# Two transformer layers on one core: where the reciprocal roots of the second attention's norms are computed

## The chip, the core and the metric

The kernel runs on one core of a Trainium2 chip, as one launch. A core has five engines with instruction queues of their own: TensorE (PE in the profile; its weight loads are PEld), VectorE (DVE), ScalarE (ACT), GpSimd (POOL) and SyncE (SP), and 16 DMA engines that all queues feed. Each engine works its queue in order, and engines wait for one another by semaphores. The metric is the device time of one execution in microseconds (us); lower is better. All data are 32-bit floats.

## What is computed

Two layers, each a cross attention and a mixture of experts, on x of 8 x 100 rows of 512, with a context of 8 x 722 rows. Cut to what matters here:

```
x = x + attention0(norm(x), context)            # 16 heads of 32, causal
x = x + experts0(norm(x))                       # 8 experts of 2048, 2 per row; has a norm of its own
x = x + attention1(norm(x), context)            # 16 heads of 64; has a norm of its own
x = x + experts1(norm(x))                       # 8 experts of 1024, 2 per row; a norm on its result
norm(x) = (x - mean(x)) / sqrt(var(x) + 1e-5)   # over the 512 columns of a row
```

Where a sublayer starts with a norm of its own, two norms follow each other on the same row. The kernel makes them in one: the variance after the first norm is known from that before it, so that the product of both factors is one reciprocal root, 1 / sqrt((1 + eps) var + eps^2).

## The kernel before

The 800 rows lie on the 128 partitions in seven tiles, the last with 32 rows (`NTILE`, `rows`, L20 and L71); x stays in SBUF throughout. The program is written in the order of the computation, a scheduler then places each engine's instructions, and that placed order is what the engines keep to.

A norm has three helpers. `moments` (L126) gives mean and variance of a tile by VectorE. `factors` (L134) makes r, the reciprocal root, and t = -mean x r: ScalarE's root (L139 for two norms in one, L141 for one), VectorE's reciprocal (L142), VectorE's product (L144). `scaled` (L147, L148) applies both to the tile on VectorE. `to_columns` (L155) turns the normed tile by TensorE (L159) and evicts it by ScalarE, plainly (L161) or with gain and shift (L168).

ScalarE looks a function up in a table, one set of which is in place at a time; where the next function needs another set, a table load stands before it (ACT_TABLE_LOAD in the trace). The root, the exponential, Gelu and Silu each bring a load when they follow one another; plain copies bring none.

Four places call `factors`. Those before the first attention (L572), before its experts (L638, L639) and on the last result (L1012) are not touched. The other two are:

- **The transition into the second attention (L732 to L744).** The experts' answers lie in DRAM in the order of experts. For each tile two gathers (`fetch`, L340, indirect DMAs that GpSimd issues) bring the two answers of each row into one of two buffers (`back0`, tag "nil"); VectorE adds them to x, weighted (L738); then come `moments`, `factors` and `scaled` (L742), the turned tile goes into `xT1` (L743), and GpSimd adds the output bias to x (L744). A gather may start when the buffer that it fills has been read. At the same time ScalarE and TensorE finish the early projections of the context (`project_early`, L725): projections (L432), their evictions by ScalarE (L436), turned values (L444, evicted at L446 to L449), and stores to DRAM that ScalarE's queue issues (L454, L464). Behind all this the first product of the attention (L760 by way of L421) needs the whole of `xT1`. One element of the last gathered tile, copied by GpSimd (L56), also holds back the loads of the next weights.
- **The second attention's output (`output`, L886).** The attention runs over 64 units, 8 batches x 8 pairs of heads. In a unit: keys projected from the context (L432, L436) or loaded, turned values (L444, L446), scores (`weighed`, L783: matmuls L793, row maximum L797 on VectorE, exponential with row sum L799 on ScalarE, reciprocal of the sums L804, spread by GpSimd L807 in the first three batches and through DRAM after them), the weights turned (`turned`, L815: L822 to L828) and the product (`attended`, L832: L843 and L847 to L850). The work is pipelined by one unit. The scores lie in two PSUM tiles, one for each head, each with a single buffer:

```python
scs = [ps_s.tile([T, 2, 512], F32, tag=f"sc{j}", name="ps_sc1") for j in range(2)]
```

so that the next unit's scores of a head can be written when the exponential of this unit has read them. When the units of all rows of a tile are done, a list of due steps (`due`, L910) puts three steps between units: `output` (product L891, sum L894, `moments`, `factors` and `scaled` into `xnf1`, L896), one unit later `logits1` (the tile turned, L159 and L161, and the router's matmuls L175), and one later `sent_on` (L903), which for groups of tiles picks the experts and sends the rows to them by indirect DMAs of GpSimd (L274). For the last two tiles no units are left to stand between.

Behind the attention, the choice of experts for the last group (L229 to L268), the order of the experts (L281 on) and the weights of the two answers (L948 to L952, with an exponential at L949) come before the experts' first rows arrive (L351). GpSimd adds the last norm's shift to x there (L1011).

Of the kernel before, what the change touches and what calls it, by code (L numbers as in the profile page):

```python
# [8 lines left out]
F32 = mybir.dt.float32  # L9
AF = mybir.ActivationFunctionType  # L10
ALU = mybir.AluOpType
AX = mybir.AxisListType

P = 128
# [15 lines left out]
EPS = 1e-5  # L30
# [36 lines left out]
def two_layers(ctx: ExitStack, tc: tile.TileContext, a: dict, out: bass.AP):  # L67
    nc = tc.nc
# [4 lines left out]
    const = ctx.enter_context(tc.tile_pool(name="const", bufs=1))  # L73
# [3 lines left out]
    def context(b, h):  # L77
        return a["ctxT"][:, b, h * (S // 2) : (h + 1) * (S // 2)].rearrange("(c p) s -> p c s", p=P)
# [9 lines left out]
    def of(layer, name, s, g):  # L88
        return lambda: a[name][bass.ds(owner[layer][s], 1), g].rearrange("o p j n -> (o p) j n")
# [13 lines left out]
    x = const.tile([P, NTILE, D], F32, name="x")  # L103
# [9 lines left out]
    eps = const.tile([P, 1], F32, name="eps")  # L113
    nc.vector.memset(eps, EPS)
    eps2 = const.tile([P, 1], F32, name="eps2")
    nc.vector.memset(eps2, EPS * EPS)
    rank = const.tile([P, NE], F32, name="rank")
    for e in range(NE):
        nc.vector.memset(rank[:, e : e + 1], float(NE - e))
# [6 lines left out]
    def moments(src, name):  # L126

        st = small.tile([P, 6], F32, tag="st", name=f"st_{name}")
        nc.vector.bn_stats(st, src)  # L129
        mv = small.tile([P, 2], F32, tag="mv", name=f"mv_{name}")  # L130
        nc.vector.bn_aggr(mv, st)
        return mv

    def factors(mv, tag, twice=False):  # L134


        r = small.tile([P, 1], F32, tag=f"r{tag}", name=f"r{tag}")
        if twice:
            nc.scalar.activation(r, mv[:, 1:], AF.Sqrt, bias=eps2, scale=1.0 + EPS)  # L139
        else:  # L140
            nc.scalar.activation(r, mv[:, 1:], AF.Sqrt, bias=eps)  # L141
        nc.vector.reciprocal(r, r)  # L142
        t = small.tile([P, 1], F32, tag=f"t{tag}", name=f"t{tag}")
        nc.vector.scalar_tensor_tensor(t, mv[:, :1], -1.0, r, ALU.mult, ALU.mult)  # L144
        return r, t

    def scaled(dst, src, r, t):  # L147
        nc.vector.tensor_scalar(dst, src, r, t, ALU.mult, ALU.add)  # L148
# [196 lines left out]
    def arrived(layer, e, r0, n, pool, psum, gamma=None, beta=None):  # L345

        xg = pool.tile([P, CAP // P, D], F32, tag="xg", name="xg")
        xT = pool.tile([P, DC, CAP], F32, tag="xgT", name="xgT")
        for s in range(-(-n // P)):
            w = min(P, n - s * P)  # L350
            nc.gpsimd.dma_start(out=xg[:w, s, :], in_=rows_of(sent, layer, e, r0 + s * P, w))  # L351
            to_columns(xT, xg[:, s, :], s * P, w, psum, gamma, beta, vector=True)
        return xT, xg
# [32 lines left out]
    def work_off(jobs, arrive, hidden, product, send_back, first=None, midway=None):  # L386


        (x, raw), done = arrive(*jobs[0][:3]), None
        if first is not None:  # L390
            weights.load(first + 8, raw[:1, 0, :1])
        for k, (e, r0, n, w1, w2) in enumerate(jobs):
            h = hidden(e, n, x, w1, lambda: done and send_back(*done))
            if k + 1 < len(jobs):
                x, raw = arrive(*jobs[k + 1][:3])
            if midway is not None and k == 4:
                midway(raw)
            done = e, r0, n, product(e, n, h, w2)
        send_back(*done)
# [71 lines left out]
    def columns_tile(name):  # L471
        return turned_x.tile([P, DC, NT], F32, tag="xT", name=name)
# [4 lines left out]
    with tc.tile_pool(name="a0", bufs=1) as ap, tc.tile_pool(name="a0w", bufs=3) as aw, tc.tile_pool(  # L477
        name="a0s", bufs=1, space=bass.MemoryType.PSUM
# [91 lines left out]
        for i in range(NTILE):  # L570
            xn = aw.tile([P, D], F32, tag="xn", name="xn0")
# [17 lines left out]
        for n in range(len(units) + 2):  # L589
            if n >= len(units) - B:  # L590
                next(steps)
            if n < len(units):
                c, b = units[n]
# [35 lines left out]
        for i in range(NTILE):  # L629
# [7 lines left out]
            mv = moments(x[:, i, :], "f0")  # L637
            scaled(xl[:, i, :], x[:, i, :], *factors(mv, "b", twice=True))  # L638
            r, t = factors(mv, "a")  # L639
# [34 lines left out]
    with f0, tc.tile_pool(name="f0w", bufs=2) as fw, tc.tile_pool(  # L674
        name="f0p", bufs=2, space=bass.MemoryType.PSUM
    ) as ps:
        cb = fp.tile([P, 2, DC, S // 2], F32, tag="xl", name="cb1")

        def fetch_context(behind):

            for h in range(2):
                nc.gpsimd.tensor_copy(cb[:1, h, 0, :1], behind[:1, 0, :1])
                nc.gpsimd.dma_start(out=cb[:, h], in_=context(1, h))

        NF = F0 // P

        def hidden0(e, n, xg, w1, between):
            h = fw.tile([P, NF, CAP], F32, tag="h", name="h0", bufs=1)
            for g in range(NF // 4):
                w = w1(g)  # L690
                for j in range(4):
                    f = 4 * g + j
                    ph = ps.tile([P, CAP], F32, tag="h", name="ps_h0")
                    for dc in range(DC):
                        nc.tensor.matmul(  # L695
                            ph[:, :n], w[:, dc, j * P : (j + 1) * P], xg[:, dc, :n],
                            start=dc == 0, stop=dc == DC - 1,
                        )
                    nc.scalar.activation(h[:, f, :n], ph[:, :n], AF.Gelu, bias=b1s[:, e, f : f + 1])  # L699
                if g == 0:  # L700
                    between()
            return h

        def work0(jobs, first=None, midway=None):
            work_off(
                jobs, lambda e, r0, n: arrived(0, e, r0, n, fw, ps, gamma0, beta0), hidden0,
                lambda e, n, h, w2: products(n, h, [w2(g) for g in range(NF // 4)], NF, fw, ps, b2s[:, e, :]),
                lambda e, r0, n, yT: returned(0, e, r0, n, yT, fp, ps), first, midway,
            )

        weights.limit = W_L1A + 4
        work0([
            (
                e, 0, CAPS[e], lambda g, k=W_L0F + 8 * e: weights.get(k + g),
                lambda g, k=W_L0F + 8 * e: weights.get(k + 4 + g),
            )
            for e in range(NE)
        ], W_L0F, fetch_context)
        rest(
            more, work0, lambda piece, e, g: piece(of(0, "W1", e, g)), lambda piece, e, g: piece(of(0, "W2", e, g)), 4  # L720
        )

        bo = fw.tile([P, D], F32, name="bo", bufs=1)
        nc.scalar.dma_start(out=bo, in_=a["bo"][0].partition_broadcast(P))
        for _ in project_early(  # L725
            1, [cb[:, h] for h in range(2)], [weights.get(W_L1A + 2 + g, 0) for g in range(2)], lambda: (
                fw.tile([P, S], F32, tag="xgT", name="mT1"), fw.tile([P, NSC, P], F32, tag="xg", name="mv1")
            ), ps, ("m", "tp"), lambda k: nc.scalar.dma_start,
        ):
            pass  # L730
        xT1 = columns_tile("xT1")
        for i in range(NTILE):  # L732
            w = rows[i]
            both = fp.tile([P, 2, D], F32, tag="nil", name="back0", bufs=2)
            for k, m in enumerate((m1, m2)):
                y = both[:, k]
                fetch(y, where, i, k)
                nc.vector.scalar_tensor_tensor(  # L738
                    x[:w, i, :], y[:w], m[:w, i : i + 1], x[:w, i, :], ALU.mult, ALU.add
                )  # L740
            xn = fp.tile([P, D], F32, tag="mv", name="xn1", bufs=2)
            scaled(xn, x[:, i, :], *factors(moments(x[:, i, :], "a1"), "b", twice=True))  # L742
            to_columns(xT1, xn, i * P, rows[i], ps, gamma1, beta1)  # L743
            nc.gpsimd.tensor_tensor(x[:, i, :], x[:, i, :], bo, ALU.add)  # L744
        weights.limit = len(pieces)
        weights.load(W_L1A + 8, y[:1, :1])


    with tc.tile_pool(name="a1", bufs=1) as ap, ExitStack() as later, tc.tile_pool(
        name="a1s", bufs=1, space=bass.MemoryType.PSUM  # L750
# [135 lines left out]
        def output(i):  # L886

            w, t0 = rows[i], i * P
            po = ps.tile([P, D], F32, tag="tp", name="ps_o1")
            for c in range(IC):  # L890
                nc.tensor.matmul(  # L891
                    po[:w], qT[:, c, t0 : t0 + w], w_o[c // 4][:, c % 4, :], start=c == 0, stop=c == IC - 1
                )
            nc.vector.tensor_tensor(x[:w, i, :], po[:w], x[:w, i, :], ALU.add)  # L894
            xn = sends[i] = aw.tile([P, D], F32, tag="xn", name="xnf1")
            scaled(xn, x[:, i, :], *factors(moments(x[:, i, :], "f1"), "a"))  # L896

        def logits1(i):
            xTf = aw.tile([P, DC, P], F32, tag="pr0", name="xTf1")
# [16 lines left out]
        for n, (b, ic) in enumerate(units):  # L916
# [7 lines left out]
            mv = values(b, ic, mT)  # L924
# [15 lines left out]
    with tc.tile_pool(name="f1", bufs=1) as fp, tc.tile_pool(name="f1w", bufs=2) as fw, tc.tile_pool(  # L940
        name="f1p", bufs=2, space=bass.MemoryType.PSUM
# [3 lines left out]
        bias = fp.tile([P, D], F32, name="bias")  # L945
# [140 lines left out]
```

## Time and profile before

| what | value |
|---|---|
| median of 3 runs (lowest, highest) | 1872.75 us (1872.5, 1874.85) |
| the profiled execution: its time, its span | 1873.61 us, 1872.1 us |
| mean granted TensorE clock | 0.962 of full speed |
| busy: TensorE, its weight loads | 1730.2 us, 1308.1 us |
| busy: VectorE, ScalarE, GpSimd | 593.0, 482.6, 151.6 us |
| table loads on ScalarE | 21, each 1283 ns |
| roots in the two touched places | 14, mean of one 287 ns (L141), 320 ns (L139) |
| mean DMA traffic | 125 GB/s |

The span runs from the first to the last instruction. The profile is one execution; times in it are from the span's start. In its rows, "idle before" is what the engine waited ahead of the instruction, and the arrow names what ended the wait. A group of instructions is given by line, engine and operation, then output and inputs by the program's names. The slices of the span show the stages: the first attention to about 150 us, the choice of its experts and their work to 630, the transition to 685, the second attention to 1480, the choice of experts to 1535, their work to 1834, and the last norm to the end.

### The profile page before, as it was taken

Reading aid. Unit: us, or ns where it says so; the run is one execution under the profiler, and the core shown is the slowest. Engines: PE = TensorE matmul, PEld = TensorE weight load, DVE = VectorE, ACT = ScalarE, POOL = GpSimd, SP = SyncE. Lnnn points to the kernel's source line nnn. Section 1 sums busy time; section 2 is a strip of 40 time slices with the busy share of each in tenths; the row PEclk is TensorE's granted clock in tenths of the full one; section 3 lists DMA queues with packets and bytes.
Section 4 is the critical chain, followed back from the end, with each engine's and each line's share of the span. In section 5 each row is a group of like instructions: output and inputs, shape, how many; then the busy total and the mean of one; then the engine's idle time right before and its main releaser. Section 6 shows DMA issues by size and latency. Waiting matters only on the chain. (4 is left out here: it accounts for less than half of the span.)

```text
span 1872.1 us, 26461 instructions
## 1 busy us (share of the span) xinstructions
PE 1730.2 (92%) x10422; PEld 1308.1 (70%) x10422; DVE 593.0 (32%) x1455; ACT 482.6 (26%) x1409; POOL 151.6 (8%) x245
## 2 busy tenths in 40 slices
PE   5999899999999879999999999999999839999990
PEld 2455579999999745666666666666666528999990
DVE  4464510111111130455444333444444331111115
ACT  2364321111111131333333323333333210010110
POOL 4010310000000130000000000000000030000003
PEclk9999999999999989999999999999999969999995
DMA  9911384465555371132010300211201145555513
GB/s 367 414 64 57 119 326 167 172 224 179 205 202 217 116 269 46 32 96 72 25 48 5 60 3 4 37 6 37 26 6 15 5 179 207 200 185 204 203 72 114
DMA packets 74982, 233.35 MB, mean 125 GB/s; under 512 B 23548, under 2 KB 35952, under 8 KB 58456
## 3 DMA queue, kind: packets, MB, share of 16 engines
q1 hardware_dynamic: 53348, 183.47, 28.4%
q0 software_dynamic: 9888, 30.06, 5.0%
q10 hardware_dynamic: 11604, 17.95, 3.1%
q8 instruction: 86, 1.41, 0.3%
q14 instruction: 56, 0.46, 0.1%
HBM read 180.41 MB, written 51.05 MB: 124 GB/s over the span
## 5 line engine op out<-in xcount | busy, mean ns | idle before, releaser
L432 PE MATMUL ps_m<-cb,w 128*128 128x361 f32 x896 | 302.4, 489 | 0.0
L363 PE MATMUL ps_y<-h,w 128*128 128x256 f32 (+7 forms) x1536 | 280.5, 344 | 0.0
L363 PEld LDWEIGHTS ps_y<-h,w 128*128 128x128 f32 x1536 | 268.6, 190 | 7.9
L432 PEld LDWEIGHTS ps_m<-cb,w 128*128 128x128 f32 x896 | 172.0, 197 | 103.7 <-issue 16.9
L695 PE MATMUL ps_h<-xgT,w 128*128 128x256 f32 (+7 forms) x1024 | 188.8, 345 | 0.0
L695 PEld LDWEIGHTS ps_h<-xgT,w 128*128 128x128 f32 x1024 | 180.3, 191 | 5.7 <-ACT h L699 0.2
L799 ACT ACTIVATE pr<-ps_sc,m 100x822 f32<-100x822 f32 x128 | 119.9, 942 | 176.2 <-DVE m L797 92.9
L797 DVE TENSOR_REDUCE m<-ps_sc 100x1 f32<-100x822 f32 x128 | 123.8, 1008 | 48.4 <-PE ps_sc L793 48.4
L823 DVE COPY prT<-ps_ptA 128x500 f32<-128x500 f32 x128 | 82.0, 678 | 178.2 <-PE ps_ptA L822 178.1
L699 ACT ACTIVATE h<-ps_h,s_b 128x256 f32<-128x256 f32 (+7 forms) x128 | 56.0, 438 | 303.6 <-PE ps_h L695 303.6
L436 ACT COPY mT<-ps_m 128x361 f32<-128x361 f32 x128 | 58.8, 460 | 254.7 <-PE ps_m L432 224.9
L421 PE MATMUL ps_col<-xT,w 128*128 128x400 f32 x320 | 115.0, 517 | 1.3 <-ACT xT L168 1.3
L965 PE MATMUL ps_g<-xgT,w 128*128 128x256 f32 (+7 forms) x512 | 104.0, 347 | 0.0
L965 PE MATMUL ps_u<-xgT,w 128*128 128x256 f32 (+7 forms) x512 | 102.8, 344 | 0.0
L421 PEld LDWEIGHTS ps_col<-xT,w 128*128 128x128 f32 x320 | 61.7, 196 | 47.4 <-issue 4.3
L965 PEld LDWEIGHTS ps_g<-xgT,w 128*128 128x128 f32 x512 | 91.2, 192 | 2.9
L793 PE MATMUL ps_sc<-mT,qT 64*100 64x411 f32 (+1 forms) x512 | 92.8, 468 | 0.0
L965 PEld LDWEIGHTS ps_u<-xgT,w 128*128 128x128 f32 x512 | 90.7, 190 | 2.6
L843 PEld LDWEIGHTS ps_av<-prT,mv 128*64 128x64 f32 (+1 forms) x1536 | 67.9, 137 | 27.2 <-issue 23.9
L970 ACT ACTIVATE sg<-ps_g 128x256 f32<-128x256 f32 (+7 forms) x64 | 22.3, 348 | 238.6 <-PE ps_g L965 238.6
L843 PE MATMUL ps_av<-prT,mv 128*64 128x100 f32 (+1 forms) x1536 | 80.6, 253 | 0.0
L822 PEld LDWEIGHTS ps_ptA<-ident,pr 100*128 100x128 f32 x640 | 65.3, 141 | 21.1 <-issue 11.0
(243 smaller groups left out, 1836.1 us busy)
## 6 DMA issues: line engine op xcount, KB each, us to landing
w<-in_W SPq DMA_DIRECT2D x64, 1024.0 KB
w<-in_w_gate SPq DMA_DIRECT2D x16, 1024.0 KB
w<-in_w_up SPq DMA_DIRECT2D x16, 1024.0 KB
w<-in_w_down SPq DMA_DIRECT2D x16, 1024.0 KB
sent<-nil SPq DMA_DIRECT2D x25, 512.0 KB
answers<-nil SPq DMA_DIRECT2D x25, 512.0 KB
cb<-in_ctxT ACTq DMA_DIRECT2D x16, 722.0 KB
mT<-kept_keys SPq DMA_DIRECT2D x13, 361.0 KB
```

What stands on the lines that cost most here:

```text
L363: nc.tensor.matmul(py[:, k, :n], ws[f // 4][:, f % 4, dc * P : (dc + 1) * P], h[:, f, :n], start=f == 0, stop=f == nf - 1,)
L421: nc.tensor.matmul(ps[:, :HALF], w[c // 4][:, dc, (c % 4) * P : (c % 4 + 1) * P], xT[:, dc, cols], start=dc == 0, stop=dc == DC - 1,)
L432: nc.tensor.matmul(pm[:, : S // 2], w_m[ic // 4][:, dc, (ic % 4) * P : (ic % 4 + 1) * P], cb[h][:, dc, : S // 2], start=dc == 0, stop=dc = ...
L436: nc.scalar.copy(mT[:, h * (S // 2) : (h + 1) * (S // 2)], pm[:, : S // 2])
L695: nc.tensor.matmul(ph[:, :n], w[:, dc, j * P : (j + 1) * P], xg[:, dc, :n], start=dc == 0, stop=dc == DC - 1,)
L793: nc.tensor.matmul(sc[:, bank, c0:c1], qT[r, ic, q0 : q0 + T], keys_, start=True, stop=True)
L797: nc.vector.tensor_reduce(m, sc[:, :, :NKH], AX.XY, ALU.max, negate=True)
L799: nc.scalar.activation(pr.rearrange("p (a n) -> p a n", a=2), sc[:, :, :NKH], AF.Exp, bias=m, accum_out=sums[:, j : j + 1],)
L822: nc.tensor.transpose(pt[:, c, :], pr[:, T + c * P : T + (c + 1) * P], ident[:T, :T])
L823: nc.vector.tensor_copy(prT[:, : NSC - 1, :], pt)
L843: nc.tensor.matmul(po[r, 0, :], vj, prT[j][:w, c, :], start=c == 0, stop=c == NSC)
L965: nc.tensor.matmul(p_[:, :n], w_[:, dc, j * P : (j + 1) * P], xg[:, dc, :n], start=dc == 0, stop=dc == DC - 1,)
```

## The change

The two touched calls of `factors` get r from GpSimd: the variance plus eps (or times 1 + eps plus eps^2), then that value to the power of -0.5, which a new constant tile holds. The second instruction takes two tensors and reads what the first wrote. ScalarE's root and VectorE's reciprocal are left out there. The other calls keep them. Lines after L142 move by up to ten in the changed file.

```diff
+    half = const.tile([P, 1], F32, name="half")
+    nc.vector.memset(half, -0.5)
...
-    def factors(mv, tag, twice=False):
+    def factors(mv, tag, twice=False, by_power=False):
...
         r = small.tile([P, 1], F32, tag=f"r{tag}", name=f"r{tag}")
-        if twice:
-            nc.scalar.activation(r, mv[:, 1:], AF.Sqrt, bias=eps2, scale=1.0 + EPS)
+        if by_power:
+            if twice:
+                nc.gpsimd.tensor_scalar(r, mv[:, 1:], 1.0 + EPS, EPS * EPS, ALU.mult, ALU.add)
+                nc.gpsimd.tensor_tensor(r, r, half, ALU.pow)
+            else:
+                nc.gpsimd.tensor_scalar(r, mv[:, 1:], EPS, None, ALU.add)
+                nc.gpsimd.tensor_tensor(r, r, half, ALU.pow)
         else:
-            nc.scalar.activation(r, mv[:, 1:], AF.Sqrt, bias=eps)
-        nc.vector.reciprocal(r, r)
+            if twice:
+                nc.scalar.activation(r, mv[:, 1:], AF.Sqrt, bias=eps2, scale=1.0 + EPS)
+            else:
+                nc.scalar.activation(r, mv[:, 1:], AF.Sqrt, bias=eps)
+            nc.vector.reciprocal(r, r)
...
-            scaled(xn, x[:, i, :], *factors(moments(x[:, i, :], "a1"), "b", twice=True))
+            scaled(xn, x[:, i, :], *factors(moments(x[:, i, :], "a1"), "b", twice=True, by_power=True))
...
-            scaled(xn, x[:, i, :], *factors(moments(x[:, i, :], "f1"), "a"))
+            scaled(xn, x[:, i, :], *factors(moments(x[:, i, :], "f1"), "a", by_power=True))
```

## The prediction

> **What bounds the kernel now.** I read the busy table first: TensorE is busy for 1730.2 of 1872.1 us, so outside a few transitions a change counts only where it alters what TensorE waits for, or the clock that it is granted. Of the norms that the change touches, seven lie in the transition into the second attention (about 640 to 685 us), seven inside and behind that attention (five at 914, 1006, 1130, 1319 and 1419 us; two at 1488 and 1504). The table of groups shows what they cost on ScalarE beside their own 0.29 us:
>
> ```profile
> L799 ACT ACT_TABLE_LOAD x6 | 7.7, 1283 | 15.1 <-issue 12.0 <-DVE m L797 3.0
> L141 ACT ACTIVATE ra<-mv_f,eps 128x1 f32<-128x1 f32 x14 | 4.0, 287 | 48.7 <-DVE mv_f L131 48.7
> ```
>
> Root and exponential need different tables, and a table load is a separate row of 1283 ns. The timeline of ScalarE at the second of the five places:
>
> ```profile
> 999.05 1.28 ACT L141 ACT_TABLE_LOAD   x1
> 1005.94 0.30 ACT L141 ACTIVATE ra<-mv_f,eps 128x1 f32<-128x1 f32 x1 [5.61 <-DVE mv_f L131]
> ...
> 1013.78 1.28 ACT L799 ACT_TABLE_LOAD   x1 [3.01 <-issue]
> 1015.07 0.95 ACT L799 ACTIVATE pr<-ps_sc,m 100x822 f32<-100x822 f32 x1
> ```
>
> The load for the root (999.05) lies in a stretch in which ScalarE had nothing to do. The load back (1013.78) does not: the exponential's row maximum was there, and the exponential began 1.28 us late. TensorE, same place:
>
> ```profile
> 1013.96 0.66 PE L159 MATMUL ps_tp<-ident,xnf 128*128 128x128 f32 x4
> 1016.16 0.41 PE L793 MATMUL ps_sc<-kT,qT 64*100 64x100 f32 x2 [1.55 <-ACT pr L799]
> 1017.09 0.41 PE L793 MATMUL ps_sc<-kT,qT 64*100 64x100 f32 x2 [0.51 <-ACT pr L799]
> 1017.71 1.48 PE L175 MATMUL ps_lg<-p_w_router,xTf 128*128 128x8 f32 x8 [0.20 <-ACT xTf L161]
> 1019.04 8.05 PE L432 MATMUL ps_m<-cb,w 128*128 128x361 f32 x16
> ```
>
> At these places no projection stands between one unit's product and the next unit's scores, so the scores wait for the exponentials to free their PSUM tile: 1.55 + 0.51 + 0.20 us idle. Elsewhere in this attention TensorE has no such gap (from 690 to 895 us it is busy for 204.37 of 205.00). And 16 projections then take 8.05 us, where the same 16 take 5.11 at 1443 us. The table by stretches says why (columns: length, PE busy, granted clock, DMA):
>
> ```profile
> 1016.00:1017.00 1.00, 0.41 (x2) 1.00 0.00 0
> ...
> 1019.00:1020.00 1.00, 1.00 (x3) 0.50 0.00 0
> 1024.00:1025.00 1.00, 1.00 (x3) 0.50 0.33 13
> 1025.00:1026.00 1.00, 1.00 (x4) 1.00 0.25 36
> ```
>
> The clock halves just behind the gap. In 14 us around each of the five places its mean is 0.76, 0.76, 0.76, 0.88, 0.88: lost are 3 x 0.24 x 14 + 2 x 0.12 x 14 = 13.4 us.
>
> **The change, part by part.** In the order in which the scheduler places the changed kernel's instructions, ScalarE loses 14 roots and 13 table loads, VectorE 14 reciprocals, GpSimd gains 14 pairs (an add, or multiply and add, and a power, 128x1 each, the second waiting for the first).
>
> *Price of a pair.* No row shows a power. Nearest are GpSimd's copy of one element, 175 ns (L56), and its two-input sum of 128x512, 1.26 us. [...] I take 0.3, near the first, since the shape is the same. From the statistics' end to t it takes 0.57 us now (914.26 to 914.83: root 0.29, reciprocal 0.17, hand-overs). New: 0.175 + 0.3 + three hand-overs of 0.05 = 0.63. [...]
>
> *The five norms within the attention.* The pair is hidden: xnf is ready at 915.57 and TensorE takes it up at 922.55, 7 us later; VectorE, which now waits in t, has 2.36 us of idle time before its next copy (L823). Without that cover, each us beyond 2.4 would be late in the next row maximum, exponential and score. GpSimd has only the L807 copies there, 18 us apart. So the load back goes at no price: 5 x 1.28 = **6.4 us**. Next late at the second place is the exponential itself: of 1.55 + 0.51 + 0.20 there remain 0.27 + 0.51 + 0.20.
>
> *The clock.* [...] I take the first place whole (its one long wait of 1.33 us vanishes: 3.4) and half of the other 10.1: **8.4 us**. Ends: 0 and 13.4.
>
> *The transition.* ScalarE's order holds it up twice:
>
> ```profile
> 643.62 1.28 ACT L139 ACT_TABLE_LOAD   x1
> 649.85 0.29 ACT L139 ACTIVATE rb<-mv_a,eps 128x1 f32<-128x1 f32 x1 [4.95 <-DVE mv_a L131]
> ...
> 672.52 5.68 ACT L168 ACTIVATE xT<-ps_tp,p_ln_b,p_ln_g 128x128 f32<-128x128 f32 x16 [0.68 <-PE ps_tp L159]
> 678.00 0.56 ACT L139 ACTIVATE rb<-mv_a,eps 128x1 f32<-128x1 f32 x2
> ```
>
> At 643 the root waits for the gathered rows and keeps the key copies behind it waiting (TensorE idle 4.62 us); at 672 sixteen evictions stand before the roots of tiles 4 and 5, whose statistics were there by 669.7, so VectorE waits 5.15 us and TensorE 3.45. Both go. In exchange GpSimd now queues four pairs between its gather DMAs: the gathers of tiles 3, 4, 5 and 6 stand behind the pairs of tiles 0, 1, 2 and 3, each of which waits for VectorE, which itself waits for gathered rows; L744's sums are spread among them too. Following that chain with 0.6 us a pair and the 3.6 us that a gather takes to land, the last tile is summed at about 671.5 us (669.6 now). The key projections end near 664 (671 now), so the first two tiles are evicted early, and from 673.4 five remain: four at 4 x 0.355 and a short one of 1.1, to 680.2. The first product (L421) starts at 680.4 in place of 685.09: **4.6 us**. It starts at half clock in both. Every 0.1 us on the power costs 0.4 here; a power of 1.3 leaves 0.6.
>
> [...]
>
> *Behind the attention.* Tiles 5 and 6 are on the path (TensorE waits 3.03 and 3.39 us for their xnf): 2 x 0.06 = 0.1 us lost; ends -0.1 and +2.1. Also VectorE's three small weights operations (L950 to L952) move ahead of the counts that TensorE waits for; at 0.16 us, partly in the gaps of dependent steps: 0.4 lost. Tile 6's pair stands ahead of L1011's seven sums, which wait for the bias DMA until 1505.81, so nothing is queued for it.
>
> Sum: 6.4 + 8.4 + 4.6 - 0.5 = 18.9 us. The profiled execution took 1873.6 (span 1872.1 and 1.5 around it), 0.9 above the median of the three runs, 1872.75. That gives 1854.7 and 1853.9; I say **1854.5**.
>
> **The rivals.** *The clock stays low, or the transition gives nothing.* [...] Without the clock's 8.4: 1863; without the 4.6: 1859; without both, 1867.5. *The power is slow.* The place is each pair, the price p. It costs 2 tails and 4 pairs on the gather chain, 6 us per us of p; beyond 2.36 us over my value the five attention norms join, 11 per us. The gain of 18.9 is used up at p = 3.1 us; at 5 us, with no clock regained, 11.7 + 9.4 + 14 - 6.4 is a loss of 29, so 1902. [...] Against: one element per lane. *The gap moves instead.* If the exponential waited for its maximum anyway, nothing would come of 6.4 and 8.4, and 1869 to 1870 be left; but the maximum's end (first of two reductions from 1012.70, some 0.97 each) is the very time at which the load began. That the loads stay is excluded by the order of instructions.
>
> **How the numbers follow.** Forecast, within 1850 to 1859: 0.50. More (all the clock back, the transition better), 1846 to 1850: 0.10. Part missing, 1859 to 1869: 0.27. Moved gap or a middling power, within 0.2% (3.7 us, about what a measurement here can tell from no change): 0.03. Slow power: 0.10. Faster is thus 0.87. The range 1848 to 1869 leaves out 0.10 above and some 0.04 below.
>
> **What would show it.** Table loads fall from 21 to 8, none between 760 and 1500 us; at the five places the wait of L793 for the exponential falls to 0.3 and 0.5 us; the granted clock in the 14 us around each is above 0.88 at three or more of them; the first L421 begins 3 to 6 us earlier after the last product of the experts' layer (now 685.1 against 630.2); a power row reads below 0.5 us. A power above 1.3 us, a pause of GpSimd before its first one, or half clock at all five places would make me wrong in size; a power above 3 us in sign.

## The result, and the profile after

| | before | after |
|---|---|---|
| median, four runs each, side by side | 1873.80 us (1872.50 to 1878.45) | 1859.27 us (1857.09 to 1860.38) |
| ratio, 95% interval | | 0.9916 (0.9899 to 0.9933) |
| the profiled execution's span | 1872.1 us | 1858.2 us |
| table loads on ScalarE | 21 | 8 |
| transition: first turned answer of the last expert to the first L421 / L431 | 54.9 us | 56.5 us |
| attention: from there to the output projection of tile 5 (L891 / L901) | 791.0 us | 776.1 us |
| from there to the experts' first rows (L159 / L169) | 55.0 us | 55.9 us |

The change made the kernel 14.5 us faster. Lines below L142 have moved by up to ten. Of the 13.9 us between the two spans, 14.9 come from the attention. The transition gave back 1.6, the part behind the attention 0.9, the rest of the program 0.9; 2.4 were gained ahead of all that the change touches; this I take for noise, since in the second trace of the same kernel, below, that part is 1.8 us longer.

First the group table of ScalarE after the change: of six loads for the exponential one is left, the first. Then that of GpSimd with the new pair's powers (columns: count, busy us and mean ns, idle time before):

```profile
L809 ACT ACT_TABLE_LOAD x1 | 1.3, 1283 | 0.0
```

```profile
L143 POOL TENSOR_TENSOR rb<-rb,half 128x1 f32<-128x1 f32 x7 | 4.3, 609 | 0.5
L146 POOL TENSOR_TENSOR ra<-ra,half 128x1 f32<-128x1 f32 x7 | 4.0, 569 | 0.6
```

Timelines of ScalarE and of TensorE at the second of the five places:

```profile
1009.64 0.95 ACT L809 ACTIVATE pr<-ps_sc,m 100x822 f32<-100x822 f32 x1 [3.02 <-issue]
```

```profile
1009.80 0.66 PE L169 MATMUL ps_tp<-ident,xnf 128*128 128x128 f32 x4
1010.74 0.41 PE L803 MATMUL ps_sc<-kT,qT 64*100 64x100 f32 x2 [0.27 <-ACT pr L809]
1011.66 0.41 PE L803 MATMUL ps_sc<-kT,qT 64*100 64x100 f32 x2 [0.51 <-ACT pr L809]
1012.28 1.06 PE L185 MATMUL ps_lg<-p_w_router,xTf 128*128 128x8 f32 x8 [0.20 <-ACT xTf L171]
```

The exponential no longer has a load in front of it, and TensorE waits 0.27 + 0.51 + 0.20 us where it waited 1.55 + 0.51 + 0.20. The stretches of 14 us around the five places (columns: length, TensorE busy, granted clock, DMA share and GB/s) show what became of the clock:

```profile
921.00:935.00 14.00, 13.96 (x98) 0.88 0.10 28
1008.00:1022.00 14.00, 13.01 (x86) 0.88 0.05 4
1129.00:1143.00 14.00, 13.01 (x104) 1.00 0.09 5
1313.00:1327.00 14.00, 13.01 (x100) 1.00 0.08 5
1410.00:1424.00 14.00, 13.01 (x86) 0.88 0.09 5
```

0.88 means one stretch of 3.4 us at half clock, which costs 1.7 us. There were eight of them before (2, 2, 2, 1, 1) and are three now: 8.5 us. Counted at full clock the attention is 6.2 us shorter, and 0.2 us less of half clock falls into its beginning: together its 14.9 us.

The transition is another matter. ScalarE and TensorE there, after the change:

```profile
660.25 13.96 ACTq L464 DMA_DIRECT2D kept_values<-mv  x2
674.25 7.10 ACT L178 ACTIVATE xT<-ps_tp,p_ln_b,p_ln_g 128x128 f32<-128x128 f32 x20 [13.88 <-DMA w<-in_Wkv]
```

```profile
675.82 1.12 PE L169 MATMUL ps_tp<-ident,xn 128*128 128x128 f32 x4 [14.62 <-ACT xT L178]
...
680.54 1.65 PE L169 MATMUL ps_tp<-ident,xn 128*128 128x128 f32 x8 [0.82 <-DVE xn L158]
684.30 4.37 PE L431 MATMUL ps_col<-xT,w 128*128 128x400 f32 x6 [2.11 <-ACT xT L178]
```

The early projections end at 659.4, where before they ended at 671.1. But then ScalarE's queue stands for 14 us at the issue of its last small store, until a load of Wkv has landed, and the evictions of the turned tiles are queued behind it. A store of `mv` does not read Wkv. The program gives its transfers eight completion semaphores in turn (in the trace, those issued by SP and ScalarE land on 100, 102 to 107 and 117); in the new order this store got 100, whose last user is the first Wkv load, so the store waits for that load, and the load is held back (L56) until the last gather. It is issued at 669.14, behind L56's copies from 668.93 on, and has landed at 673.88; the store goes out at 673.96.

### The profile page after: what moved, and what is told of

It is laid out like the page before. It is cut to its first block, busy times and chain, and to the rows that moved or that the text cites. A ratio compares the mean times of both kernels' runs of the same rounds, so it can differ in the third digit from the quotient of the medians.

```text
span 1858.2 us, 26462 instructions
## 1 busy us (share of the span) xinstructions
PE 1718.6 (92%) x10422; PEld 1300.8 (70%) x10422; DVE 587.7 (32%) x1442; ACT 462.3 (25%) x1382; POOL 164.8 (9%) x273
## 5 line engine op out<-in xcount | busy, mean ns | idle before, releaser
L442 PE MATMUL ps_m<-cb,w 128*128 128x361 f32 x896 | 294.0, 478 | 0.0
L442 PEld LDWEIGHTS ps_m<-cb,w 128*128 128x128 f32 x896 | 167.6, 192 | 99.9 <-issue 10.2
L431 PE MATMUL ps_col<-xT,w 128*128 128x400 f32 x320 | 114.8, 517 | 2.1 <-ACT xT L178 2.1
L431 PEld LDWEIGHTS ps_col<-xT,w 128*128 128x128 f32 x320 | 61.7, 196 | 48.1 <-issue 4.0
L803 PE MATMUL ps_sc<-mT,qT 64*100 64x311 f32 (+1 forms) x512 | 92.2, 468 | 0.0
```

Of the source, the lines that this page charges most:

```text
L431: nc.tensor.matmul(ps[:, :HALF], w[c // 4][:, dc, (c % 4) * P : (c % 4 + 1) * P], xT[:, dc, cols], start=dc == 0, stop=dc == DC - 1,)
L442: nc.tensor.matmul(pm[:, : S // 2], w_m[ic // 4][:, dc, (ic % 4) * P : (ic % 4 + 1) * P], cb[h][:, dc, : S // 2], start=dc == 0, stop=dc = ...
L803: nc.tensor.matmul(sc[:, bank, c0:c1], qT[r, ic, q0 : q0 + T], keys_, start=True, stop=True)
```

## The experiments

Every trace is cut at the same four points. "At full clock" is a stretch's length less what half clock took in it (the sum of (1 - granted clock) x length over stretches of 2 us). "Falls" counts stretches of 3.4 us at half clock at the five places. Ratios are to the kernel before, run on the same chip beside each; its own medians there were 1873.80 to 1877.34, so kernels are to be compared by their ratios.

| kernel | median us (runs) | ratio, 95% | transition | attention | at full clock | falls |
|---|---|---|---|---|---|---|
| before | 1873.80 (4) | | 54.9 | 791.0 | 774.7 | 8 |
| the change | 1859.27 (4) | 0.9916 (0.9899, 0.9933) | 56.5 | 776.1 | 768.5 | 3 |
| after_again | 1862.15 (6) | 0.9919 (0.9903, 0.9936) | 57.1 | 772.4 | 768.6 | 1 |
| f1_only | 1864.23 (6) | 0.9951 (0.9936, 0.9967) | 56.2 | 771.8 | 768.3 | 1 |
| a1_only | 1874.71 (13) | 1.0002 (0.9994, 1.0010) | 56.4 | 790.7 | 774.4 | 8 |
| f1_copy | 1859.01 (6) | 0.9936 (0.9918, 0.9953) | 56.8 | 773.1 | 769.0 | 1 |
| f1_both | 1874.72 (10) | 0.9996 (0.9983, 1.0010) | 57.4 | 788.2 | 774.9 | 6 |
| delay1 | 1871.01 (12) | 0.9970 (0.9957, 0.9984) | 57.0 | 783.1 | 772.3 | 5 |
| delay2 | 1881.01 (10) | 1.0020 (1.0006, 1.0035) | 57.0 | 787.7 | 775.9 | 6 |
| lane_sp | 1862.28 (5) | 0.9936 (0.9923, 0.9949) | 55.6 | 781.4 | 768.2 | 6 |
| sums | 1859.64 (4) | 0.9924 (0.9900, 0.9948) | 55.0 | 775.1 | 768.4 | 3 |
| lane_sums | 1859.82 (6) | 0.9909 (0.9890, 0.9928) | 51.0 | 784.6 | 770.8 | 7 |
| lane_sums2 | 1855.61 (5) | 0.9891 (0.9871, 0.9911) | 50.7 | 772.4 | 768.7 | 1 |
| lane_fill | 1853.72 (4) | 0.9879 (0.9860, 0.9898) | 50.5 | 772.5 | 769.5 | 0 |

### Which half of the change gives the gain

f1_only and a1_only leave the power in one of the two calls:

```diff
# f1_only
-            scaled(xn, x[:, i, :], *factors(moments(x[:, i, :], "a1"), "b", twice=True, by_power=True))
+            scaled(xn, x[:, i, :], *factors(moments(x[:, i, :], "a1"), "b", twice=True))
# a1_only
-            scaled(xn, x[:, i, :], *factors(moments(x[:, i, :], "f1"), "a", by_power=True))
+            scaled(xn, x[:, i, :], *factors(moments(x[:, i, :], "f1"), "a"))
```

f1_only, expected:

> The power only for the norm behind the attention (tag f1, lines L145 and L146); the transition keeps ScalarE's roots. My theory: the gain sits in the attention alone (first query projection matmul to the last tile's output projection, 791.0 us before, 776.1 with both powers), and the transition (first gather of the answers' rows at 630 to the first query projection, 54.9 before) is as before. So attention 776 +- 2, transition 55 +- 1, time ratio to before 0.991 to 0.993 (about 15 to 16 us less, 0.9 back behind the attention), that is as fast as or 1.6 us faster than the whole change. Rival, that the transition's power gives part of the gain: the ratio stays at 0.994 or above.

a1_only, expected:

> The power only for the norm ahead of the attention (tag a1, lines L142 and L143); roots on ScalarE behind it as before. My theory: the transition alone changes, and it becomes 1.6 us longer (56.5 instead of 54.9), because ScalarE's last small store of the early projections then stands about 14 us at the semaphore of a Wkv weight load; the attention keeps its 791. Ratio to before 1.000 to 1.002. Rival, my forecast: 4.6 us shorter, ratio 0.9975.

a1_only settles it: 1.0002, and an attention of 790.7 us as before. The power in the transition is worth nothing in time; it makes the transition 56.4 to 57.4 us in the seven traces that have it without another edit there, where the two with roots show 54.9 and 56.2. The gain is that of the other call. f1_only's trace says so (771.8 us, 768.3 at full clock), though its transition, 56.2 us, is just above the 55 +- 1 that I expected. Its median does not reach the ratio that I expected, and by the letter falls on the rival's side: its six runs spread from 1857.5 to 1868.4 us, with mean granted clocks from 0.968 down to 0.961, a difference that is worth 13 us in 1860. Only the fastest has a trace. So a1_only excludes that the transition's power gains by itself; that both halves act on each other by way of the clock is not excluded.

### Loads, or work taken off ScalarE

```diff
# f1_copy, in place of the pair
+                nc.scalar.activation(r, mv[:, 1:], AF.Identity, bias=eps)
+                nc.vector.reciprocal(r, r)
# f1_both, behind the pair
+                nc.scalar.activation(idle, mv[:, 1:], AF.Sqrt, bias=eps)
```

f1_copy, expected:

> As the whole change, but behind the attention an Identity activation of ScalarE with the reciprocal of VectorE stands in the place of the GpSimd pair (the root itself is left out there, so no table is loaded). Theory (the gain of the attention is the five table loads and the TensorE clock lost with them; that GpSimd makes the power gives nothing): attention 776 +- 2, and the 0.9 us lost behind the attention come back to 0.0 to 0.5 (hand-over mv to t about 0.57 instead of 1.01). Ratio to before 0.990 to 0.992. Rival (taking work off ScalarE's queue is what helps, not the loads): attention 780 or more.

f1_both, expected:

> As the whole change, with a ScalarE square root added behind each GpSimd pair of the norm behind the attention, whose result nobody reads: the table loads come back, the power stays. Theory (the loads are the cause): the attention counted at full clock is 774 to 775 as before (768.5 with the change), the lost half clock comes back at all five places (13 to 14 us beside the 2.5 of the start), attention 789 to 792, ratio to before 0.999 to 1.003. Rival (the gain comes from the root's work leaving ScalarE and VectorE's reciprocal): attention under 780.

f1_copy keeps an operation of ScalarE and VectorE's reciprocal, but loads no table (it leaves the root out, so its norm is another one): 769.0 at full clock. Its ratio, 0.9936, misses the 0.990 to 0.992 that I expected: four of its runs took 1856 to 1859 us and two 1866 to 1867. f1_both has the power and the loads: 774.9, and every one of the five places falls, with six stretches where I expected eight. Its ScalarE rows, from the timeline at the second place:

```profile
1001.81 1.28 ACT L148 ACT_TABLE_LOAD   x1
...
1008.70 0.29 ACT L148 ACTIVATE idle<-mv_f,eps 128x1 f32<-128x1 f32 x1 [5.61 <-DVE mv_f L133]
...
1016.54 1.28 ACT L811 ACT_TABLE_LOAD   x1 [3.01 <-issue]
```

So it is the load back; the traces show no sign of anything else about the root. That GpSimd makes the power gives nothing in itself.

### The load, or the length of the gap

```diff
# delay1, in weighed, once behind each output(i); delay2: two operations, 100x822 and 100x512
+                    nc.scalar.activation(
+                        pr[:, :512].rearrange("p (a n) -> p a n", a=2), sc[:, :, :256], AF.Identity, bias=m)
```

delay1, expected:

> As the whole change, with one idle ScalarE operation (100x512, about 0.5 us) ahead of the first exponential behind each of the five output projections in the attention. The full-clock length of the attention should be 768.5 + 5 x 0.5 = 771. Theory of the gate (a place loses 1.7 us of clock for each 3.4 us stretch that a thin gap trips, and the longer the gap, the surer it trips; with the change, traces so far show 1, 1, 3 and 6 stretches at the five places where before had 8): more stretches than the change's mean of 2.75, 4 to 8 of them, median time 1866 to 1872. Rival (the table load itself, not the length of the gap, draws the clock down): 1 to 3 stretches, attention 774 to 779.

delay2, expected:

> As the whole change, with two idle ScalarE operations (100x822 and 100x512, about 1.35 us together) ahead of the first exponential behind each of the five output projections: about the length of a table load, but no table is loaded. Theory (a load costs its length and, through the longer gap, the clock; nothing else about it matters): attention at full clock 775 to 776.5, half clock at all five places (5 to 8 stretches of 1.7 us), ratio to before 0.999 to 1.003. Rival (the load itself draws the clock down): 0 to 3 stretches, ratio under 0.996.

Idle operations of about a load's length do what the load did: 775.9 at full clock, 7.4 more than the change, which is 1.5 for each place (they put the exponential off by 1.57 us at the second place, somewhat more than a load), and six falls, at four of the five places. The half dose adds 3.8 (0.76 for each place; I had said 0.5, but the operation takes 0.69 us from start to end) and five falls. The rival, that a table load draws the clock down in another way, is out.

### Why the clock is not the same from run to run

> The whole change once more, beside the other three on the same chip, for the spread: attention at full clock 768.5 again, half clock at the five places anything from 1 to 6 stretches, transition 56 to 57, times from 1856 to 1867. Rival (its four times of 1857 to 1860 are all there is): within 1857 to 1861 and 3 stretches.

The change again, unaltered: at full clock 768.6 as in its first trace, but one fall instead of three, and times from 1859.0 to 1865.8. What varies in the attention is only the clock. In one trace all its steps lie on one grid: read in stretches of 0.1 us, the change's clock comes back up at 689.3, 928.3, 1017.0 and 1419.8, that is 70, 26 and 118 times 3.41 us apart. In all 14 traces the recorded steps keep such a grid, 3.413 us wide, to within 1 ns; where it lies against the program differs from trace to trace.

Laid on this grid, TensorE's poorest stretch at each of the five places in the trace of before has it busy for 0.38 to 0.61, and half clock follows in the next stretch (at the fourth place in the one after that). Over all traces: with a load or delay2, 19 places of 20 fall; with delay1, 4 of 5; with the short gap, 19 of 40 (the change twice, f1_only, f1_copy, sums, lane_sp, lane_sums, lane_sums2).

With the short gap the busy share does not tell which. Here are the stretch with the gap and the one behind it, at the second place, first in f1_only and then in sums (columns: length, TensorE busy, granted clock, DMA share and GB/s):

```profile
1011.38:1014.80 3.42, 2.70 (x16) 1.00 0.03 0
1014.80:1018.21 3.41, 3.41 (x13) 1.00 0.00 0
```

```profile
1008.96:1012.37 3.41, 2.69 (x16) 1.00 0.03 0
1012.37:1015.78 3.41, 3.41 (x7) 0.50 0.00 0
```

At the first place of the change, of lane_sp and of lane_sums, half clock even followed a stretch in which TensorE was busy for 0.99. What does tell them apart is the work in the stretch. I count a matmul's moving columns, times the share of 128 x 128 that its weights fill (in a row with 64*100 64x311 the weights are 64*100 and 311 columns move). Back-to-back projections then make 3860 in a stretch (16 x 361 in 5.11 us); a router matmul makes 8 and a score matmul of 64x100 makes 39, in about 0.13 and 0.2 us, in which projections would make 150 and 230. By this count the two stretches above have 1559 and 1226. Of the 70 places (five in each of 14 traces) 42 fell: the stretch ahead of the fall has 173 to 1396 in 41 of them and 1493 in one (delay2, second place). The poorest stretch at the 28 others has 1442 or more. In the 3133 stretches of the 14 attentions (their ends left out) the next stretch is at half clock below some 1440 and at full clock above, with that one exception; the return to full clock follows the same count.

So where the gap and the thin matmuls around it fall on the grid decides, and a shift of 0.3 us, as between f1_only and sums, is enough. The count was found in the traces afterwards, and no run moved the gap on purpose. What exactly the clock counts stays open: behind the attention, where the last output tile has weights of 128x32, stretches of 450 to 1000 kept full clock or regained it. With rows alone as the share, eight of 7382 stretches from 30 to 1830 us go against a bound of 1526.

### The transition: two covers

```diff
# lane_sp: the last 82x128 store leaves ScalarE's queue
+        nc.sync.dma_start(out=last_store[0][0], in_=last_store[0][1])      # behind the Wkv loads
# sums: the sums leave the loop, and are tied behind the last pair
-            nc.gpsimd.tensor_tensor(x[:, i, :], x[:, i, :], bo, ALU.add)   # in the loop over tiles
+        nc.gpsimd.tensor_copy(bo[:1, :1], r[:1])
+        nc.sync.dma_start(out=bo, in_=a["bo"][0].partition_broadcast(P))
+        for i in range(NTILE):
+            nc.gpsimd.tensor_tensor(x[:, i, :], x[:, i, :], bo, ALU.add)
# lane_sums: both.  lane_sums2: both, with bo loaded early and tied by an operation instead:
+        nc.gpsimd.tensor_scalar(bo[:1, :1], bo[:1, :1], r[:1], r[:1], ALU.add, ALU.subtract)
```

lane_sp, expected:

> Both powers, and the last small store of the early projections (82x128 of kept_values) is issued by SP behind the Wkv loads and no longer by ScalarE. Theory (ScalarE's queue, with the tile transposes' copies behind it, stands from 660.3 to 674.2 at that store): the copies of tiles 0 to 2 now run before 665, the transition becomes 50 to 53 us instead of 56.5, and the time is 3 to 6 us below the whole change, ratio to before 0.988 to 0.990. Rival (the chain of gathers, power pairs and sums on GpSimd ends the transition whatever ScalarE does): transition 56 +- 0.5, ratio 0.992 as the whole change.

ScalarE no longer stood, and yet the transition took 55.6 us; the rival had it. VectorE's and GpSimd's timelines in lane_sp:

```profile
675.34 0.16 DVE L154 SCALAR_TENSOR_TENSOR tb<-mv_a,rb 128x1 f32<-128x1 f32 x1 [3.27 <-POOL rb L143]
676.25 0.16 DVE L154 SCALAR_TENSOR_TENSOR tb<-mv_a,rb 128x1 f32<-128x1 f32 x1 [0.75 <-POOL rb L143]
...
679.21 0.16 DVE L154 SCALAR_TENSOR_TENSOR tb<-mv_a,rb 128x1 f32<-128x1 f32 x1 [2.27 <-POOL rb L143]
```

```profile
671.70 1.50 POOL L760 TENSOR_TENSOR x<-x,bo 128x512 f32<-128x512 f32 x1 [0.98 <-DVE xn L158]
673.26 0.19 POOL L142 TENSOR_SCALAR rb<-mv_a 128x1 f32<-128x1 f32 x1
673.53 1.26 POOL L760 TENSOR_TENSOR x<-x,bo 128x512 f32<-128x512 f32 x1
674.75 0.56 POOL L143 TENSOR_TENSOR rb<-rb,half 128x1 f32<-128x1 f32 x1
```

A pair of 0.19 + 0.56 us takes from 673.26 to 675.31, because a sum of 1.26 us stands between its two instructions and another before them. The same three waits (3.27, 0.75, 2.27 us) stand in the change's own trace, hidden there under ScalarE's.

sums, expected:

> As the whole change, with the sums x+bo behind the last power pair, but ScalarE's last store where it was, at a Wkv load's semaphore. Theory of the two covers: ScalarE still stands until about 674 and then has all seven tiles' copies to make (about 10 us), so the transition stays at 55.5 to 57 us though VectorE no longer waits for the pairs. Rival (the sums alone were to blame): 50 to 52.

lane_sums, expected:

> As lane_sp, and the seven sums x+bo of the transition stand behind the last power pair in GpSimd's queue (bo is loaded behind it). In lane_sp the copies of tiles 0 and 1 did run early, and yet the transition took 55.6 us: the pairs of the last three tiles stood behind sums, and VectorE waited 3.3, 0.8 and 2.3 us for them. Theory (two covers, each of which hides the other: ScalarE's store, and the sums ahead of the pairs): with both gone the transition becomes 49.5 to 52 us (56.5 with the whole change), the three waits for rb fall under 1.2 us each. Rival (the gathers' data end the transition in any case): 55 to 57. The attention counted at full clock stays at 768 to 769.

The sums alone: 55.0 us, half a microsecond below what I expected, and ScalarE takes up the first eviction at 675.50. Both together: 51.0 us. Against the 56.4 to 57.4 us of the traces with both covers, taking away one gains 1 to 2 us and taking away both 6. lane_sums lost 2.3 us of it again at the start of the attention: bo came late, the sums that wait for it ended at 690.7, and SP's queue, with ScalarE's behind it, stood until then.

lane_sums2, expected:

> As lane_sums, but bo is loaded early as in the change and not behind the pairs: in lane_sums that late load held SP's and then ScalarE's queue until 690.7, and TensorE waited 1.9 us and more for the query copies in the first 20 us of the attention. Theory: transition 50 to 52 us as in lane_sums, attention at full clock back at 768 to 769 (770.8 in lane_sums), so about 5 us below the whole change where the clock draws are equal; with draws of 3 to 13 us in the attention a median of 1850 to 1860. Rival (the sums, now at 675 to 684, hold the first transfers of the attention as the late bo did): 770 or more.

Both covers gone, and the attention at 768.7 at full clock. VectorE's waits and TensorE's rows:

```profile
673.64 0.16 DVE L154 SCALAR_TENSOR_TENSOR tb<-mv_a,rb 128x1 f32<-128x1 f32 x1 [0.72 <-POOL rb L143]
...
674.55 0.16 DVE L154 SCALAR_TENSOR_TENSOR tb<-mv_a,rb 128x1 f32<-128x1 f32 x1 [0.53 <-POOL rb L143]
...
676.11 0.16 DVE L154 SCALAR_TENSOR_TENSOR tb<-mv_a,rb 128x1 f32<-128x1 f32 x1 [0.94 <-POOL rb L143]
```

```profile
672.61 1.94 PE L169 MATMUL ps_tp<-ident,xn 128*128 128x128 f32 x8 [9.18 <-DVE xn L158]
...
680.64 1.70 PE L431 MATMUL ps_col<-xT,w 128*128 128x400 f32 x2 [1.92 <-ACT xT L178]
```

The gathered rows bound it now, by way of VectorE's order: the normed tile for which TensorE waits 9.18 us is made when VectorE has added up the last gathered rows, which stand ahead of it in its queue.

### Filling the gap

```diff
# lane_fill = lane_sums2 and, in logits1 behind to_columns:
+            idle = ps.tile([P, 512], F32, tag="tp", name="ps_idle")
+            for k in range(2):
+                nc.tensor.matmul(idle[:, :400], ident, sends[i][:, :400], start=True, stop=True)
```

> As lane_sums2, with two idle matmuls (128x400, 0.5 us each) behind the transposes of the router's columns at each of the seven output tiles, so that TensorE works through most of the gap at the five places; two score matmuls that stood in the gap move behind. Theory (a stretch of the clock grid falls when TensorE had too little work in the one before): the five places lose 0 to 1 stretches instead of 1 to 6, the attention at full clock grows by 0 to 4 us (5 x 0 to 0.8), so attention 772 to 776, with little spread from run to run. Rival (the clock falls whatever fills the gap): 2 to 6 stretches, attention 778 to 785.

The idle matmuls' result is read by nobody. Two pairs of short score matmuls, which in lane_sums2 stood in the gap at the second place and waited 0.27 and 0.51 us there, are now placed behind the projections, so this kernel both fills the gap and takes two waits out of it. TensorE at the second place, and the clock around all five:

```profile
1006.73 1.51 PE L923 MATMUL ps_idle<-xnf,ident 128*128 128x400 f32 x4
1008.71 1.06 PE L185 MATMUL ps_lg<-p_w_router,xTf 128*128 128x8 f32 x8 [0.47 <-ACT xTf L171]
1009.63 5.11 PE L442 MATMUL ps_m<-cb,w 128*128 128x361 f32 x16
```

```profile
915.00:929.00 14.00, 13.75 (x125) 1.00 0.11 28
1002.00:1016.00 14.00, 13.53 (x101) 1.00 0.04 0
1123.00:1137.00 14.00, 13.52 (x98) 1.00 0.08 5
1307.00:1321.00 14.00, 13.52 (x101) 1.00 0.07 3
1404.00:1418.00 14.00, 13.53 (x103) 1.00 0.09 2
```

No fall at any place, for 0.8 us more at full clock than lane_sums2; the poorest stretch at the five places has 2181 to 2551 columns of work. The 16 projections behind the gap take 5.11 us, full speed. The four times lie within 1853.3 and 1857.2, and the mean granted clocks of the three runs without a trace, 0.967 to 0.969, are no lower than the traced one's, 0.966. It is the fastest kernel here, 8.4 us below the change on the same chip (1853.72 against 1862.15, and their intervals do not touch). Against lane_sums2 alone the difference is not settled, in the median or in the spread: the intervals overlap, its five times lie within 1853.2 and 1862.4, and the two traces have the same attention, 772.4 and 772.5 us. What the new order would do without the idle matmuls was not run.

## Why the prediction was right, and where it was not

**The load back at five places: right.** 6.4 us were said; at full clock the attention lost 6.2 (774.7 to 768.5). The waits left over, 0.27, 0.51 and 0.20, are those forecast. f1_copy, f1_both and delay2 show that the load's length was at work, and show nothing besides.

**The clock: the size right by luck, the places wrong.** 8.4 us said, 8.5 measured in the trace. I gave the first place back whole and half of the rest; that half was an estimate for which no run shows a reason. In fact the first place kept one fall, the third and fourth kept none. And 8.4 is not a property of the kernel: the change's second trace regained 11.9 (one fall instead of eight), and the same attention in lane_sums only 1.7. The ends that I gave, 0 and 13.4, were the honest part. Idle time of TensorE did not tell where the clock came down: no stretch was idle, in the change's trace TensorE was busy for 0.99, 0.71 and 0.71 of those ahead of the falls at the first, second and fifth place, and half clock came. In the trace of before, 1.33 us of idle time at the first place was followed by two stretches of half clock, and 1.55 us at 663, more, by none:

```profile
664.99 0.66 PE L444 MATMUL ps_mv<-ident,mT 128*128 128x128 f32 x4 [1.55 <-ACT mT L436]
```

```profile
924.53 0.41 PE L793 MATMUL ps_sc<-kT,qT 64*100 64x100 f32 x2 [1.33 <-ACT pr L799]
```

The count of work, in which a score matmul of 64x100 makes 39 and a router matmul 8 where projections would make 230 and 150, did tell, in the attentions. A gap reduced to 1 us did not leave the clock up (19 of 40 places fell); it left it to where the gap fell on the grid, which differed between traces. With the gap filled and two waits gone it stayed up, five of five in the one trace.

**The transition: the step that failed.** The prediction had 4.6 us gained (its own end points, 685.09 and 680.4, give 4.7); 1.6 were lost in this trace. That the gain did not come is shown; the loss is not, since f1_only, with the roots kept there, took 56.2 us. The step "the key projections end near 664, so the first two tiles are evicted early, and from 673.4 five remain" fell at its second half. The projections ended sooner still, but no tile was evicted before 674, because ScalarE's queue stood at a store. I had counted what ScalarE would compute and not the transfers that it issues, which wait too. The second miss stood behind it: "L744's sums are spread among them too" was said and not priced, and VectorE waited 6.3 us in all for three pairs that stood among sums. With both out of the way the first L421 comes 50.5 to 51.0 us after the experts' last product, 3.9 to 4.4 sooner than in the trace of before: about what I had promised for the change itself. My figure for the gathers' end (671.5) was on the late side; the last pair of gathers was summed at 669.7.

**The power: dearer than said, and it did not matter.** 0.57 us for the power instead of 0.3, and from the statistics to t 1.0 us instead of 0.63:

```profile
1488.29 0.18 DVE L133 BATCH_NORM_AGGREGATE mv_f<-st_f 128x2 f32<-128x6 f32 x1
1489.47 0.16 DVE L154 SCALAR_TENSOR_TENSOR ta<-mv_f,ra 128x1 f32<-128x1 f32 x1 [1.00 <-POOL ra L146]
```

At the five places 7 us of cover hide it, as said. A power of 1.3 us, with which the end of +2.1 behind the attention was worked out, is shown by no run: in the change's trace 13 of the 14 powers took 0.55 to 0.58 us and one 0.90. A pause of GpSimd before its first one is not shown either: that pair, at 650.46, took 0.40 and 0.58 us.

**Behind the attention: 0.9 lost, 0.5 said.** The longer pair would explain it: 2 x 0.44 instead of 2 x 0.06, and the 0.4 for VectorE's small operations is then not needed. f1_copy, which has no pair there, took 55.1 us as before. I do not call it shown, since the kernels with the pair spread from 55.4 to 59.0 in this part.

The sum was 18.9 where 14.5 were measured. Of the difference, 4.6 is the transition's term; its loss of 1.6 more and the 2.4 gained ahead of the touched code nearly cancel.

## What to carry to other kernels

Before costing a step that ends sooner, list everything that its engine has queued behind it, the transfers that it issues above all: each can wait for a transfer that it does not read (here for 13.9 us). When taking a wait away brings nothing, look for a second one under it before giving up the first: here each of two repairs alone was worth 1 to 2 us, and both together six. And where a thin gap sets the granted clock, count the work that falls into one stretch of the clock's grid, not TensorE's busy time, and give the gap's worth as a range over executions; or fill the gap, which cost 0.8 us here and left no fall in the one trace taken.

## What the runs showed of the hardware

- In the trace of before, a table load of 1283 ns stands ahead of ScalarE's first root and at each of the 20 changes among root, exponential, Gelu and Silu behind it, and none at a plain copy.
- In the change's trace a GpSimd power of 128x1 took 0.55 to 0.58 us in 13 of 14 (the maximum was 0.90), the operation before it 0.19 to 0.25 in 12 of 14 (the maximum was 0.53); between VectorE's statistics and its next step at 1488 the pair cost 0.44 us more than a root with a reciprocal (1.00 against 0.56).
- Half clock came in stretches of 3.413 us on one grid that held over a whole execution, and it followed stretches in which TensorE was busy for as much as 0.99. In the attentions of all 14 traces it followed those with less than about 1440 columns of work by the count above, where projections at full speed make 3860; one of 3133 stretches is an exception. So two traces of the change, 768.5 and 768.6 us at full clock, took 776.1 and 772.4 us.
- Idle matmuls, with two waits moved out of the gap, left no fall at the five places of lane_fill's one trace, for 0.8 us at full clock. A net gain over the same kernel without them is not shown.
